# Four-layer sparse graph attention: seven row gathers of the third layer placed behind the gathers of packed queries

## Chip, cores and metric

One core of one Trainium2 chip runs the whole kernel. The metric is device time in microseconds (us). Three runs of the kernel before gave 1655.29, 1661.34 and 1661.87 us, median 1661.34. A profiled execution of the same kernel took 1662.6 us, and its instructions span 1660.9 us, so 1.7 us lie outside the span.

## What is computed

Eight batches of 2048 nodes with 64 features pass through four layers of graph attention over one sparse adjacency matrix (about 1 edge in 500 set, more for the nodes with low numbers). Each layer is `x = x + layer(relu(layernorm(x)))`. The layer concerned here is layer 2, the one with four heads:

```python
mask = graph + jnp.eye(N, dtype=graph.dtype) > 0
h = jnp.einsum('bnc,hdc->bhnd', x, Wh)
out_h = _gat_layer(h, mask[None, None], bh[None, :, None, :])   # softmax(h h^T, masked) h + b
cat = jnp.transpose(out_h, (0, 2, 1, 3)).reshape(B, N, H * D)
z = jax.nn.leaky_relu(cat, negative_slope=0.2)
h2 = jnp.einsum('bnk,dk->bnd', z, Wo)
out2 = _gat_layer(h2, mask[None], bo)                            # then leaky, layernorm, add to x
```

## The kernel before

**Tiles and slots.** The nodes are cut into 16 tiles of 128. The kernel does not form the 2048 x 2048 scores. For tile `i`, each query keeps its first `ROWS[i]` neighbours in slots of its own, and what neighbours are left over are packed, 128 at a time, into `PACKED[i]` further slots. One slot is one indirect DMA of 128 rows (`gather`, L252 to 264, the DMA at L259) from a table in HBM into one of the 26 places of a ring in SBUF (`RING`, `ring`, `held`). A tile has `ROWS[i] + PACKED[i]` slots: 4 each for tiles 8, 9 and 10, 3 each for 12, 11 and 13, and 17 for tile 0.

**The heads' stage of layer 2.** `ORDER2` (L44) names the tiles in the order 8, 9, 10, 12, 11, 13, 0, 7, and so on. `pipeline(take2, first2, second2, third2, fourth2)` at L858 walks over them, tile n being taken while tile n-1 is scored and n-2 is weighed.

- `take2` (L744 to 752) gathers the tile's rows, loads the tile's own rows and its projected queries `q` (1 MB, L751), and asks `fetch` for the first packed queries.
- `fetch` (L735 to 742) sends indirect DMAs `qe` (L740), 128 projected queries of 8,320 bytes each, about 1.06 MB, for the packed slots of all tiles in one stream. There are `QE = 4` buffers, so the fifth `qe` can go only when VectorE has done with the first. Scoring a packed slot asks for the `qe` four places on (L773). What follows call these qe0, qe1, ... : qe0 is that of tile 8, qe1 of tile 9, qe2 of tile 10, qe3 and qe4 of tile 12.
- `score` (L754 to 773): for each slot ScalarE copies the row into PSUM (L763), VectorE multiplies it with the query (L765, 2.28 us), sums over features (L769, 2.29 us) and subtracts (L770), and ScalarE takes the exponential (L771).
- `weights` (L775 to 798), twice a tile: GpSimd multiplies rows by weights (L782, 1.92 us each; L795 adds two such products), TensorE sums them in PSUM (L797); `divided` scales the sums on ScalarE (L805).
- `third2` and `fourth2` project them (L830 to 854, VectorE's part at L451), and store the rows of the table that layer 2's second half gathers from.

The projected queries are made by `products` (L330 to 345), the last stage of layer 1, which stores them into the table `qtab` (L345). A `qe` reads any row of `qtab`, so qe0 must wait until the last tile's store has landed. A row gather of layer 2 must wait for the last store into `table[2]` (L363), which comes earlier.

**What sets the order of the queues.** Each engine runs its instructions in the order of its own queue. That order is fixed when the program is built, by a planner that walks through the program with a clock of its own: of the instructions whose inputs are there by that clock it takes the one that comes first in the program text. An instruction that is not ready is passed over, and later ones go ahead of it. A gather is ready as soon as its table is stored and its place in the ring is free. GpSimd's queue carries all row gathers, all `qe`, and all of L782 and L795.

In layers 1 and 3 the function `additive` already holds gathers back: the gather of tile n waits for the scoring of tile n-3 (`SPREAD`, L516 to 518). In the heads' stage nothing holds them back.

Of the kernel before, what the change touches and what calls it, by code (L numbers as in the profile page):

```python
# [34 lines left out]

PAIRS = [0, 0, 2, 2, 2, 0, 0, 0, 2, 2, 2, 2, 2, 2, 2, 2]
QE = 4

SPREAD = 3

# [21 lines left out]
def edge_stack(ctx: ExitStack, tc: tile.TileContext, x_in, adj, w1, w1t, a1, wh, wht, bh, wo, bo,  # L62
# [9 lines left out]
    nc = tc.nc  # L72
# [143 lines left out]
    order = list(MAKING)  # L216
# [35 lines left out]
    def gather(k, i, st, behind=None):  # L252

        n = SLOTS[i]
        assert sum(SLOTS[j] for j in held) + n <= RING
        held[i], front[0] = front[0], (front[0] + n) % RING
        cols = table[k].shape[1]
        for t in range(n):
            g = nc.gpsimd.indirect_dma_start(  # L259
                out=ring[:, (held[i] + t) % RING, :cols], out_offset=None, in_=table[k][:, :],  # L260
                in_offset=bass.IndirectOffsetOnAxis(ap=idx[:, OFF[i] + t:OFF[i] + t + 1], axis=0))
            if behind is not None and t == 0:
                tc.add_manual_dep(g.ins, behind.ins.name, mybir.DependencyInfo(
                    mybir.DependencyClass.Sync, mybir.DependencyReason.DATA), reason="gather")

    def load(st, name, src, bufs):
        st[name] = rows_pool[0].tile([P, F], F32, name=name, bufs=bufs)
        nc.sync.dma_start(out=st[name], in_=src)

    def rows_of(k, i):  # L270
        return table[k][i * P:(i + 1) * P, :F]
# [452 lines left out]
    with tc.tile_pool(name="l2", bufs=2) as l2p, \  # L724
# [5 lines left out]
        thin[0] = ps_z  # L730

        stream = [(i, t) for i in order for t in range(PACKED[i])]
        sent = {}

        def fetch(upto):  # L735

            while len(sent) <= min(upto, len(stream) - 1):
                i, t = stream[len(sent)]
                q = sent[i, t] = l2p.tile([P, QW], F32, name="qe", bufs=QE)
                nc.gpsimd.indirect_dma_start(  # L740
                    out=q, out_offset=None, in_=qtab[:, :],
                    in_offset=bass.IndirectOffsetOnAxis(ap=qidx[:, POFF[i] + t:POFF[i] + t + 1], axis=0))

        def take2(i, st):  # L744
            gather(2, i, st)
            load(st, "rows", rows_of(2, i), 3)
            if i in order[:2]:
                st["q"] = kept[i]
            else:
                st["q"] = own_pool[0].tile([P, QW], F32, name="q")  # L750
                nc.sync.dma_start(out=st["q"], in_=qtab[i * P:(i + 1) * P, :])  # L751
            fetch(stream.index((i, 0)) + min(PACKED[i], QE) - 1)

        def score(i, st, lo, hi):  # L754

            K, n = ROWS[i], hi - lo
            w = l2p.tile([P, max(ROWS), B * H], F32, name="w2", bufs=5)[:, :n]
            st.setdefault("w", []).append(w)
            s = ps_s.tile([P, F], F32, name="s2")[:, :n * B * H].rearrange("p (t c) -> p t c", c=B * H)
            for t in range(lo, hi):  # L760
                q = st["q"] if t < K else sent[i, t - K]
                g = ps_g.tile([P, F], F32, name="g2")
                nc.scalar.copy(g, row(i, t))  # L763
                pr = l2p.tile([P, B * H, D], F32, name="prod2")
                nc.vector.tensor_tensor(  # L765
                    pr.rearrange("p (b h) d -> p b h d", h=H),
                    q[:, :B * H * D].rearrange("p (b h d) -> p b h d", h=H, d=D),
                    heads(g)[:, :, None, :].to_broadcast([P, B, H, D]), op=OP.mult)
                nc.vector.tensor_reduce(s[:, t - lo, :], pr, AX.X, OP.add)  # L769
                nc.vector.tensor_tensor(s[:, t - lo, :], s[:, t - lo, :], q[:, B * H * D:], op=OP.subtract)  # L770
                nc.scalar.activation(w[:, t - lo], s[:, t - lo], AF.Exp, bias=mbb[:, OFF[i] + t:OFF[i] + t + 1])  # L771
                if t >= K:
                    fetch(stream.index((i, t - K)) + QE)  # L773

# [66 lines left out]
        def fourth2(i, st):  # L841
# [14 lines left out]
            store_rows(3, i, h2, False)  # L856

        pipeline(take2, first2, second2, third2, fourth2)  # L858
        thin[0] = None
    own.close()  # L860
# [543 lines left out]
def whole_stack(tc, t, out):  # L1404
    nc = tc.nc
    D = t["gamma"].shape[0]
    with tc.tile_pool(name="flag", bufs=1) as pool:
        flag = pool.tile([1, 1], I32, name="flag")
        edge_stack(tc, t["x"], t["adj"], t["w1"], t["w1t"], t["a1"], t["wh"], t["wht"], t["bh"], t["wo"],
                   t["bo"], t["gamma"], t["beta"], t["w3"], t["w3t"], t["a3"], out, flag)  # L1410
        bad = nc.values_load(flag, min_val=0, max_val=1)
        with tc.If(bad > 0):
            gnn_stack(tc, t["x"].rearrange("n (b d) -> n b d", d=D), t["adj"], t["w1"], t["a1"], t["wht"],
                      t["bh"], t["wo"], t["bo"], t["gamma"], t["beta"], t["w3"], t["a3"],
                      out.rearrange("n (b d) -> n b d", d=D))
# [36 lines left out]
```

## Time and profile before

| | us |
|---|---|
| Median of three runs | 1661.34 |
| Profiled execution | 1662.6 |
| Its span | 1660.9 |
| VectorE (DVE) busy | 1311.9 (79%) |
| TensorE (PE) busy | 1214.6 (73%) |
| GpSimd (POOL) busy | 1151.1 (69%) |
| ScalarE (ACT) busy | 741.6 (45%) |
| L259, row gathers on POOL, 405 of them | 396.2 busy, 222.4 idle before them |
| L782, row times weight on POOL, 162 of them | 307.3 busy, 30.0 idle before them |
| L740, packed queries on POOL, 32 of them | 0.94 to 0.98 each |

The heads' stage lies between 636 us (its first gather) and 1193 us (the first gather of the next stage). In a timeline line the columns are the start in us, the length in us, the engine, the line of the kernel, the operation, what it writes and reads, the count, and in brackets the idle time ahead of it and what ended that. An indirect DMA shows twice: the POOL instruction (about 0.95 us) that issues it, and the transfer, which lands later.

### The profile page before, as it was taken

What the parts mean: (1) busy time and instruction counts of PE and PEld (TensorE: products, weight loads), DVE (VectorE), ACT (ScalarE), POOL (GpSimd) and SP (SyncE); (2) the same over time, 40 slices, a digit from 0 to 9 for tenths busy, and PEclk for the clock granted to TensorE, in tenths of its full rate; (3) what the DMA queues carried; (4) which work ended last, traced back from release to release, by engine and by line L of the source; (5) the groups of instructions that cost most, each with busy time, mean ns of one, the idle gap of its engine ahead of it and who ended that gap; (6) DMA issues with size and microseconds to landing.
All of it is one profiled execution on the core that took longest, in us unless ns stands there. A gap on an engine that the chain in (4) does not pass through costs nothing. (4 is left out here: it accounts for less than half of the span.)

```text
span 1660.9 us, 15702 instructions
## 1 busy us (share of the span) xinstructions
PE 1214.6 (73%) x3771; PEld 606.7 (37%) x3771; DVE 1311.9 (79%) x2674; ACT 741.6 (45%) x2362; POOL 1151.1 (69%) x903
## 2 busy tenths in 40 slices
PE   0025576776789974599997999999576868846898
PEld 0012243343454541234343344443233424423555
DVE  5978999994669987799999799861179979954667
ACT  5851223443257783356632455554334445560011
POOL 5765866786764215899689889998277889656650
PEclk9998877986889997799999999999877978857899
DMA  5545554453776537656255345300273443126771
GB/s 167 181 163 179 171 191 164 140 193 125 213 256 231 183 157 271 233 180 222 92 202 184 123 142 188 138 13 13 102 259 121 146 127 114 64 77 198 228 213 63
DMA packets 85787, 266.94 MB, mean 161 GB/s; under 512 B 14627, under 2 KB 14659, under 8 KB 75446
## 3 DMA queue, kind: packets, MB, share of 16 engines
q0 software_dynamic: 37328, 141.05, 27.4%
q1 hardware_dynamic: 48358, 124.79, 21.0%
q8 instruction: 32, 0.52, 0.1%
q14 instruction: 69, 0.57, 0.1%
HBM read 208.74 MB, written 57.05 MB: 160 GB/s over the span
## 5 line engine op out<-in xcount | busy, mean ns | idle before, releaser
L259 POOL DMA_INDIRECT g<-table,idx x405 | 396.2, 978 | 222.4 <-issue 131.7
L782 POOL TENSOR_TENSOR wh<-g,w 128x1024 f32<-128x1024 f32 x162 | 307.3, 1917 | 30.0 <-PE y L797 27.9
L394 PE MATMUL y<-wg,ident 128*128 128x512 f32 x392 | 232.4, 720 | 74.4 <-POOL wg L389 67.8
L299 POOL TENSOR_TENSOR ln_r<-ln_q,mhalf 128x8 f32<-128x8 f32 x80 | 135.9, 1702 | 129.0 <-DVE ln_q L297 93.0
L769 DVE TENSOR_REDUCE s<-prod 128x32 f32<-128x2048 f32 x81 | 183.9, 2285 | 14.6 <-ACT w L771 14.4
L389 POOL TENSOR_TENSOR wg<-g,w 128x1024 f32<-128x1024 f32 (+1 forms) x91 | 160.0, 1767 | 39.7 <-ACT w L445 31.7
L797 PE MATMUL y<-wh,ident 128*128 128x512 f32 x320 | 154.3, 609 | 28.1 <-POOL wh L795 24.4
L394 PE MATMUL y<-wg,selt 128*128 128x512 f32 x256 | 142.7, 669 | 6.0 <-POOL wg L389 6.0
L394 PEld LDWEIGHTS y<-wg,ident 128*128 128x128 f32 x392 | 79.6, 223 | 160.4 <-POOL wg L389 82.8
L797 PE MATMUL y<-wh,selt 128*128 128x512 f32 x256 | 124.6, 613 | 10.4 <-POOL wh L782 10.4
L805 ACT ACTIVATE yn<-y,rec 128x64 f32<-128x64 f32 x512 | 110.7, 366 | 27.6 <-PE y L797 26.8
L765 DVE TENSOR_TENSOR prod<-q,g 128x2048 f32<-128x2048 f32 x49 | 111.4, 2274 | 5.2 <-ACT g L763 5.1
L389 DVE TENSOR_TENSOR wg<-g,tiny 128x1024 f32<-128x1024 f32 (+1 forms) x92 | 98.1, 1086 | 12.3 <-PE y L394 11.9
L451 DVE SCALAR_TENSOR_TENSOR zt<-m,bhc,att 128x512 f32<-128x512 f32 x64 | 47.2, 737 | 74.9 <-ACT att L450 74.8
L408 PE MATMUL m<-w,selt 128*128 128x8 f32 (+1 forms) x384 | 61.0, 262 | 54.0 <-ACT w L554 19.1
L408 PEld LDWEIGHTS m<-w,selt 128*128 128x128 f32 x384 | 63.7, 215 | 100.0 <-ACT w L554 26.6
L307 ACT ACTIVATE xh<-x,ln_r 128x64 f32<-128x64 f32 x256 | 88.2, 427 | 25.5 <-POOL ln_r L301 25.4
L797 PEld LDWEIGHTS y<-wh,ident 128*128 128x128 f32 x320 | 58.9, 193 | 104.1 <-issue 64.4
L763 ACT COPY g<-g 128x512 f32<-128x512 f32 x81 | 50.4, 622 | 98.6 <-DVE prod L765 92.6
L437 PE MATMUL q<-rows,sel 128*128 128x512 f32 x128 | 81.4, 739 | 15.4 <-DVE prod L431 8.0
L765 DVE TENSOR_TENSOR prod<-qe,g 128x2048 f32<-128x2048 f32 x32 | 73.0, 2281 | 15.6 <-DMA qe<-qtab,qidx 14.5
L315 PE MATMUL q<-ident,xh 128*128 128x128 f32 x192 | 51.3, 341 | 44.9 <-ACT xh L307 43.1
(208 smaller groups left out, 2593.9 us busy)
## 6 DMA issues: line engine op xcount, KB each, us to landing
qtab<-q SPq DMA_DIRECT2D x16, 1040.0 KB, 4.0
a<-in_adj_dram SPq DMA_DIRECT2D x16, 1024.0 KB, 7.2
q<-qtab SPq DMA_DIRECT2D x14, 1040.0 KB, 5.3
table<-xh SPq DMA_DIRECT2D x48, 256.0 KB, 2.0
rows<-table SPq DMA_DIRECT2D x48, 256.0 KB, 3.8
xs<-x SPq DMA_DIRECT2D x48, 256.0 KB, 2.1
x<-xs SPq DMA_DIRECT2D x48, 256.0 KB, 3.6
table<-xh SPq DMA_DIRECT2D x32, 260.0 KB, 2.4
```

What stands on the lines that cost most here:

```text
L259: g = nc.gpsimd.indirect_dma_start(out=ring[:, (held[i] + t) % RING, :cols], out_offset=None, in_=table[k][:, :], in_offset=bass.IndirectO ...
L299: nc.gpsimd.tensor_tensor(st["rstd"][:, 0, :], q, mhalf, op=OP.pow)
L307: nc.scalar.activation(dst[:, b * D:(b + 1) * D], st["src"][:, b * D:(b + 1) * D], func, bias=0.0 if st["less"] is None else r[:, 1, b:b + ...
L389: eng.tensor_tensor(wg[:, :m].rearrange("p t (b d) -> p t b d", b=B), g[:, :, :F].rearrange("p t (b d) -> p t b d", b=B), w[:, t0:t0 + m, ...
L394: nc.tensor.matmul(y, lhs(i, t), wg[:, t - t0, :], start=(t == 0 and own is None), stop=(t == n - 1))
L408: nc.tensor.matmul(p[:, :cols], selt(i, t), packed[:, t, :], start=(t == 0), stop=(t == T - 1))
L437: nc.tensor.matmul(qe, sel(i, t - K), q, start=True, stop=True)
L765: nc.vector.tensor_tensor(pr.rearrange("p (b h) d -> p b h d", h=H), q[:, :B * H * D].rearrange("p (b h d) -> p b h d", h=H, d=D), heads(g ...
L769: nc.vector.tensor_reduce(s[:, t - lo, :], pr, AX.X, OP.add)
L782: nc.gpsimd.tensor_tensor(wg, heads(row(i, t))[:, :, None, :].to_broadcast([P, B, 2, D]), w[:, :, 2 * k:2 * k + 2, None].to_broadcast([P, ...
L797: nc.tensor.matmul(st["ys"][j], lhs(i, t), wg[:, 4 * j:4 * j + 4], start=False, stop=(t == n - 1))
L805: nc.scalar.activation(yn[:, b, h, :], st["ys"][j][:, b, h, :], AF.Copy, scale=st["rec"][:, 4 * j + b, 2 * k + h:2 * k + h + 1])
```

## The change

The change touches the heads' stage alone. `fetch` now remembers the last `qe` that it issued (`newest`). `take2` notes after each tile which `qe` that was (`lately`). For the third and the fourth tile in the order (n = 2 and 3, tiles 10 and 12), the gathers are written inside `tc.issue_after(...)` of the note left two tiles earlier. `issue_after` is an edge in the queue's order only: the gathers must stand behind that `qe` in GpSimd's queue; they do not wait for it to land. Gathers of the other tiles carry no such edge, and no instruction is added or removed.

```diff
 QE = 4
+LATER = 4
...
-        sent = {}
+        sent, newest, lately = {}, [None], []
 
         def fetch(upto):
...
-                nc.gpsimd.indirect_dma_start(
+                newest[0] = nc.gpsimd.indirect_dma_start(
...
         def take2(i, st):
-            gather(2, i, st)
+
+            n = order.index(i)
+            with tc.issue_after(lately[n - 2].ins) if 2 <= n < LATER else nullcontext():
+                gather(2, i, st)
             load(st, "rows", rows_of(2, i), 3)
...
             fetch(stream.index((i, 0)) + min(PACKED[i], QE) - 1)
+            lately.append(newest[0])
```

At tile 8 `fetch` sends one `qe`, so `lately[0]` is qe0, and the four gathers of tile 10 stand behind qe0. Before tile 9 is taken, the scoring of tile 8's packed slot has asked for four further ones, so `lately[1]` is qe4, and the three gathers of tile 12 stand behind qe4. "Layers 1 and 3 spread" in the change's name is what `SPREAD` does already; it is the same in both kernels.

## Prediction

> **What bounds the kernel now.** The change touches one stage, so I looked first at busy time by stretch of the heads' stage (columns: stretch, length, then PE, PEld, DVE, ACT and POOL busy with counts, granted PE clock, DMA share, GB/s).
>
> ```profile
> 636.00:668.00 32.00, 8.47 (x15) 2.74 (x13) 22.86 (x18) 6.59 (x13) 24.25 (x26) 0.65 0.91 327
> 668.00:684.00 16.00, 2.58 (x3) 1.17 (x4) 7.32 (x5) 1.10 (x2) 12.28 (x10) 0.50 0.82 307
> 684.00:790.00 106.00, 98.23 (x278) 41.97 (x277) 100.78 (x91) 62.75 (x215) 99.36 (x64) 0.99 0.57 192
> 790.00:866.00 76.00, 72.22 (x215) 31.97 (x214) 74.54 (x60) 36.94 (x107) 56.09 (x34) 1.00 0.41 140
> 866.00:943.00 77.00, 61.58 (x146) 25.29 (x145) 64.48 (x55) 26.86 (x86) 70.89 (x49) 0.96 0.48 155
> ```
>
> Read columns DVE and POOL. From 684 to 790 both are full: DVE 100.8 of 106, POOL 99.4. From 790 to 866 DVE alone is full (74.5 of 76), and POOL has 20 us to spare. From 866 to 943 POOL is full. So the stage changes its bound twice. Next I asked the timeline where the start loses time.
>
> ```profile
> 661.91 0.26 DVE L412 TENSOR_REDUCE row<-w 128x32 f32<-128x96 f32 x1 [0.35 <-ACT w L771]
> 676.65 2.29 DVE L765 TENSOR_TENSOR prod<-qe,g 128x2048 f32<-128x2048 f32 x1 [14.48 <-DMA qe<-qtab,qidx]
> ```
>
> ```profile
> 636.13 1.02 POOL L259 DMA_INDIRECT g<-table,idx  x1 [5.75 <-DMA table<-xh]
> ...
> 667.48 0.94 POOL L259 DMA_INDIRECT g<-table,idx  x1 [0.30 <-issue]
> 668.72 0.94 POOL L740 DMA_INDIRECT qe<-qtab,qidx  x1 [0.30 <-issue]
> ...
> 673.42 5.64 POOL L782 TENSOR_TENSOR wh<-g,w 128x1024 f32<-128x1024 f32 x3
> 679.03 2.34 POOL L795 TENSOR_TENSOR wh<-wh 128x1024 f32<-128x1024 f32 x1
> 683.83 0.97 POOL L740 DMA_INDIRECT qe<-qtab,qidx  x1 [2.47 <-DVE s L770]
> 684.83 5.65 POOL L782 TENSOR_TENSOR wh<-g,w 128x1024 f32<-128x1024 f32 x3
> ```
>
> DVE stands still 14.48 us for qe0. Between 636 and 668 POOL issues 26 gathers, 1.25 us apart: the ring's 26 places, tiles 8, 9, 10, 12, 11, 13 (21) and the first five of tile 0. Only then come qe0 to qe3. Was qe0's data there earlier? The waits of SP's queue answer.
>
> ```profile
> SPq L751 <- DVE s L770: 7.4, 1, 7.4
> SPq L751 <- DMA qtab<-q: 3.9, 1, 3.9
> ```
>
> The load at L751 went at 661.59; less 7.4, the last store into `qtab` had landed by 654.2. So qe0 stood in the queue 14.5 us longer than its data asked, as long as DVE's stall.
>
> [...] at 683.83 POOL had stood 2.47 us for DVE's L770. [...] at a DMA share of 0.91 the last `qtab` store took 7.7 us (646.49 to 654.2), where the page of the profile has a median of 4.0. [...] the trace has a median of 6.1 us for a `qe`, but 6.0 to 13.7 for the first five, so I use 7.93 us, from qe0's issue (668.72) to DVE's start (676.65).
>
> **The change part by part.**
>
> *Seven gathers leave the place ahead of qe0.* Four of tile 10, three of tile 12. The other 19 carry no edge, and the trace shows that the planner brings every gather with a free place ahead of a `qe` that isn't ready, even tile 0's. I expect 19 ahead: 636.13 + 19 x 1.25 = 659.9 us for qe0, 8.8 us earlier than 668.72. The store (654.2) is not the limit. DVE starts at 659.9 + 7.93 = 667.8, and its stall is 676.65 - 667.8 = 8.8 us shorter. Bounds: nothing, if the order stays; 14.5 us, if only tiles 8 and 9 stay ahead.
>
> *The seven come back behind.* They are not removed. POOL's queue becomes: 19 gathers to 659.9; qe0 to qe3, 4 x 1.25, to 664.9; tile 10's gathers to 669.9; four L782/L795 operations, 5.64 + 2.34, to 677.9; then qe4. It needs L770 of qe0, which comes 6.9 us after DVE's start (676.65 to 683.56), so at 674.7: POOL no longer waits. With issue, qe4 is done at 679.1, tile 12's gathers take 3.75, and the next L782 starts at 682.8, against 684.83. **POOL gains 2.0 us**, its removed wait of 2.5 less roundings, not 8.8. If tile 12's gathers fall between later products, the first of these starts up to 3.75 us sooner and those after it give that back.
>
> *What is late next.* POOL then runs to 789 with one gap of 0.51 us, issue gaps apart. DVE's lead of 8.8 us can't stay, because ScalarE ties them: the scaled sums (L805), which need POOL's products through PE, stand in its queue ahead of the copies and exponentials that DVE needs. At 716 it shows:
>
> ```profile
> 709.45 0.69 ACT L450 ACTIVATE att<-m,bhl 128x512 f32<-128x512 f32 x1 [0.33 <-PE m L834]
> 716.06 1.74 ACT L805 ACTIVATE yn<-y,rec 128x64 f32<-128x64 f32 x8 [4.01 <-PE y L797]
> 717.64 0.34 ACT L771 ACTIVATE w<-s,mbb 128x32 f32<-128x32 f32 x1
> ```
>
> The exponential at 717.64 already cost DVE 1.27 us (718.01). Part of this chain is DVE's own: L451 at 713.80 reads what ACT had finished at 710.14, PE's L846 waits for it, and PE's packed sum (L797) stands behind L846 at 714.90, while POOL had its product at 712.4 (the first of three from 710.50, 1.92 each). So PE could be 2.4 us earlier without POOL. I take a lead of **2.0 + 2.4 = 4.4 us**; the other 4.4 of the 8.8 return as waits on ACT. From 790 to 866 POOL waits 11.0 us for DVE (`qe`) and 8.0 for PE (L797), so there POOL can make up the 2.4. Beyond 866 both are shifted alike, and the next stage begins when the last row of this one is stored: a shift passes on whole.
>
> *Hidden, costed at nothing.* Tile 10's rows now land by 669.9 + 13.7 = 684 at the latest measured landing; ACT copies the first at 695.57, less 8.8: 686.8. The cover is 3 us; gone, it costs the lateness on DVE. Tile 12's rows (682.8 + 8) are first needed about 714. The edge is no wait; behind qe4 in the queue stand POOL's products, and PE waits for those, but qe4 is ready 3 us before POOL reaches it. SP's queue has nothing moved.
>
> **Sum.** 1662.6 - 4.4 = 1658.2 for the profiled execution. This lies 1.3 above the median of the runs, so against the median: 1661.3 - 4.4 = **1656.9 us**, 0.26% less.
>
> **Rivals.** What a measurement of this kernel can tell from no change is about 0.5%, 8.3 us.
>
> *Full gain.* DVE is the bound and keeps 8.8: 1652.5; up to 14.5 with eight gathers ahead: 1646.8. For it: DVE idles only 5.2 us in 684 to 790. Against: POOL is as full there.
>
> *POOL waits instead: slower.* Place: POOL's queue ahead of qe0. If the planner doesn't bring tiles 11, 13 and 0 forward past the held ones, eight gathers end at 646.1, POOL idles 8.0 us to 654.2, and the 11 gathers (13.75 us) fall into the full stretch. By 789 the same work is done with 8.0 - 2.5 = 5.5 us more idle: 1666.8. It decides from 2.5 us of idle, that is with fewer than 12 gathers ahead (636.1 + 12 x 1.25 = 651.1; 654.2 - 2.5 = 651.7). The same happens if qe4 is placed ahead of the four products. For it: the trace shows hoisting without edges only.
>
> *The planner's order shifts elsewhere.* Seven moved instructions change its clock; ties fall otherwise on PE, ACT and POOL over 530 us. The stall at 912 (9.93 us, DVE for ACT's L771, POOL behind it) shows what one unlucky place costs: 1661 plus or minus 10. The change's own effect is then not what shows.
>
> **How the numbers follow.** Absorbed gain 0.49, centre 1656.9, own range 1652 to 1661. Full gain 0.16, of which 0.11 beyond 8.3 us and 0.04 below 1649. POOL waits 0.20, of which 0.08 above 1669.6, where the idle also hits products that PE needs. Order shifts 0.15, of which 0.03 more than 8.3 us faster and 0.09 more than 8.3 us slower. The forecast's own case reaches past the lower bound with 0.01, since the runs before scatter by 6.6 us. Faster: 0.11 + 0.03 + 0.01 = 0.15; slower: 0.08 + 0.09 = 0.17; same: the other 0.68. The range 1649 to 1669 leaves out 0.04 of full gain and 0.01 of shifts below, and 0.08 of waits and about 0.07 of shifts above, 0.20 in all.
>
> **What would show it.** Right: 19 gathers ahead of the first `qe`, that at about 660; DVE's wait for it 5 to 7 us; a new wait of 4 us in all on ACT's L763 or L771 between 685 and 720; POOL's product that was at 684.83 at 681 to 683. Wrong: fewer gathers ahead with POOL idle before 654; POOL's waits for DVE from 790 to 866 gone by 8 us or more (full gain); DVE's stall unchanged; or layer 2 elsewhere in another order.

## The result, and the profile after

| | us | ratio to the kernel before (95% interval) |
|---|---|---|
| Before, 10 runs | 1661.3 | |
| Changed, 10 runs | 1666.78 | 1.0032 (1.0018 to 1.0046) |
| Forecast | 1656.9 | 0.9974 |

The changed kernel is 0.32% slower, 5.5 us. The time lies inside the range (1649 to 1669), but only because the range also had to hold the rivals: the sign is not the one forecast. The profiled execution took 1668.23 us with a span of 1666.5 us.

The place of the change looks as forecast. First the timeline of the changed kernel on GpSimd (all lines stand one to five numbers later than before):

```profile
633.15 1.02 POOL L260 DMA_INDIRECT g<-table,idx  x1 [6.30 <-DMA table<-xh]
...
655.74 0.94 POOL L260 DMA_INDIRECT g<-table,idx  x1 [0.30 <-issue]
656.98 0.94 POOL L741 DMA_INDIRECT qe<-qtab,qidx  x1 [0.30 <-issue]
...
661.95 0.95 POOL L260 DMA_INDIRECT g<-table,idx  x1 [0.30 <-issue]
...
666.69 5.64 POOL L787 TENSOR_TENSOR wh<-g,w 128x1024 f32<-128x1024 f32 x3
672.29 2.34 POOL L800 TENSOR_TENSOR wh<-wh 128x1024 f32<-128x1024 f32 x1
674.79 0.98 POOL L741 DMA_INDIRECT qe<-qtab,qidx  x1 [0.16 <-issue]
...
679.54 5.65 POOL L787 TENSOR_TENSOR wh<-g,w 128x1024 f32<-128x1024 f32 x3
```

That is: nineteen gathers, qe0 to qe3, four gathers of tile 10, the products, qe4 without a wait, three gathers of tile 12, products. On VectorE the stall for qe0 has gone from 14.48 to 4.83 us:

```profile
665.12 2.29 DVE L770 TENSOR_TENSOR prod<-qe,g 128x2048 f32<-128x2048 f32 x1 [4.83 <-DMA qe<-qtab,qidx]
```

To see where the time is lost I cut both profiled executions at three marks that each timeline shows: the first gather of the heads' stage, the load of `sel` with which the second half of layer 2 starts, and the last store of row maxima, after which only layer 3 is left.

| us | up to the heads | heads' stage | second half of layer 2 | layer 3 |
|---|---|---|---|---|
| before | 636.13 | 556.93 | 306.72 | 161.12 |
| changed | 633.15 | 556.56 | 311.38 | 165.41 |

The heads' stage gains only 0.4 us, and 9 us are lost behind it, where no instruction was touched. (The 3 us ahead of the stage are scatter of single executions: up to there both kernels run the same instructions in the same order.) The two traces also show that the order of the queues differs from the heads' stage on. In the second half of layer 2, counted by source line, VectorE's queue has an instruction of another line in 284 of its 493 places, ScalarE's in 117 of 465, TensorE's in 223 of 580, GpSimd's in 48 of 175. The planner walks through the program with one clock, so seven gathers that it places otherwise can move every later choice.

What that costs is in the groups of VectorE in the second half of layer 2 (busy us and mean ns behind the bar). Before:

```profile
L297 DVE TENSOR_SCALAR ln_q<-ln_q 128x8 f32<-128x8 f32 x32 | 12.7, 396 | 0.2
L280 DVE TENSOR_SCALAR tiny<-ln_s 128x8 f32<-128x8 f32 x32 | 5.1, 159 | 0.0
```

After:

```profile
L298 DVE TENSOR_SCALAR ln_q<-ln_q 128x8 f32<-128x8 f32 x32 | 19.8, 618 | 0.2
L281 DVE TENSOR_SCALAR tiny<-ln_s 128x8 f32<-128x8 f32 x32 | 5.1, 160 | 0.1
```

These are two operations of the same kind on 128x8 values. The one that writes to PSUM (`tiny`) takes 160 ns both times. The one that stays in SBUF (`ln_q`, mean times 1/64 plus epsilon in `norm_b`) takes 396 ns on average before and 618 after, 7.1 us more, on the engine that is busiest there (246.4 us of the 306.7 before). All other groups of VectorE agree within 0.3 us. The mean hides two kinds: 24 of the 32 take 150 to 223 ns before, and 8 take 0.52 to 1.85 us. After, 11 take more than 0.3 us, up to 3.46. The timeline of the changed kernel shows the longest one, all engines together:

```profile
1354.57 0.95 POOL L260 DMA_INDIRECT g<-table,idx  x1 [0.30 <-issue]
1355.02 3.46 DVE L298 TENSOR_SCALAR ln_q<-ln_q 128x8 f32<-128x8 f32 x1
...
1355.53 2.91 POOL L390 TENSOR_TENSOR wg<-g,w 128x512 f32<-128x512 f32 x2
...
1358.39 0.69 DVE L904 TENSOR_TENSOR y<-y,bo_b 128x512 f32<-128x512 f32 x1
```

It begins while GpSimd issues a gather, and ends at 1358.48, when GpSimd's two products have just ended (1355.53 + 2.91 = 1358.44). No wait is shown; the time is booked as busy. The other long ones end in the same way. In the profile of before, 8 of the 32 begin while GpSimd is at a product (L389): they are the 8 long ones, and each ends 26 to 41 ns after a product or a sum of GpSimd has ended. None of the other 24, among them 6 that begin during the issue of a gather, takes more than 223 ns. After, 10 of the 11 long ones end 26 to 40 ns behind a product or a sum, the eleventh (360 ns) with the issue of a gather. `tiny` meets a product as often (10 of 32 both times), and none of the 32 takes more than 171 ns.

The traces show when `ln_q` stands still, not what stops it. Beside GpSimd's other small operation, `ln_r` on 128x8 values (L299, L300), an `ln_q` of this stage that began in the middle of it took at most 174 ns before (8 of them) and 177 after (10). My guess, which the experiments below test, is that `ln_q` stands still while GpSimd is at a product or a sum, and that it would not in a form that also writes an extra sum. If it is so, the order that the planner picks decides how often, and for how long, these small operations meet GpSimd's products.

### The profile page after: what moved, and what is told of

Same layout as the page of the kernel before. It is cut to its first block, busy times and chain, and to the rows that moved or that the text cites. A ratio compares the mean times of both kernels' runs of the same rounds, so it can differ in the third digit from the quotient of the medians.

```text
span 1666.5 us, 15695 instructions
## 1 busy us (share of the span) xinstructions
PE 1229.8 (74%) x3771; PEld 614.1 (37%) x3771; DVE 1325.0 (80%) x2674; ACT 742.6 (45%) x2362; POOL 1152.4 (69%) x903
## 4 chain that ended last, share of the span: by engine, by line
PE 25%; DVE 13%; POOL 7%; ACT 6%; issue 5%; DMA 5%; SPq 0%; POOLq 0%; DVEq 0%; ACTq 0%
PE y L802 10%; PE y L395 5%; POOL g L260 3%; ACT yn L810 3%; DVE s L774 3%; DVE prod L770 3%; PE y L794 2%; PE m L851 2%; DMA g<-table,idx 2%; DMA rows<-table 2%; PE m L839 2%; POOL wh L787 2%; POOL wg L390 1%; POOL ln_r L300 1%; PE m L835 1%
## 5 line engine op out<-in xcount | busy, mean ns | idle before, releaser
L395 PE MATMUL y<-wg,ident 128*128 128x512 f32 x392 | 245.8, 760 | 66.5 <-POOL wg L390 56.2
L300 POOL TENSOR_TENSOR ln_r<-ln_q,mhalf 128x8 f32<-128x8 f32 x80 | 135.9, 1702 | 131.0 <-DVE ln_q L298 95.5
L395 PEld LDWEIGHTS y<-wg,ident 128*128 128x128 f32 x392 | 85.7, 239 | 158.5 <-POOL wg L390 73.6
L390 DVE TENSOR_TENSOR wg<-g,tiny 128x1024 f32<-128x1024 f32 (+1 forms) x92 | 98.1, 1085 | 16.7 <-PE y L395 16.4
L794 PE MATMUL y<-rows,ident 128*128 128x512 f32 x128 | 70.9, 641 | 19.3 <-DMA rows<-table 12.9
L369 POOL TENSOR_TENSOR acc<-acc,xh 128x512 f32<-128x512 f32 x45 | 58.4, 1299 | 31.0 <-ACT xh L308 22.3
```

The costliest lines, as they stand in the source:

```text
L300: nc.gpsimd.tensor_tensor(st["rstd"][:, 0, :], q, mhalf, op=OP.pow)
L390: eng.tensor_tensor(wg[:, :m].rearrange("p t (b d) -> p t b d", b=B), g[:, :, :F].rearrange("p t (b d) -> p t b d", b=B), w[:, t0:t0 + m, ...
L395: nc.tensor.matmul(y, lhs(i, t), wg[:, t - t0, :], start=(t == 0 and own is None), stop=(t == n - 1))
L794: nc.tensor.matmul(st["ys"][j], ident, xb[:, 4 * j:4 * j + 4], start=True, stop=False)
```

## The experiments

All were run on other chips, where the kernel before takes about 1705 us (medians 1703.75 to 1706.62 in four sessions). Every ratio is to the kernel before in the same session, with its 95% interval. To hold an order I chained each engine's instructions of a stage by edges that fix the queue's order only, as `issue_after` does; the order itself is that of the kernel before or of the changed one. The traces show the queues in the order that was asked for:

```diff
+def pinned(tc, nc, text):
+    by = {i.name: i for i in nc.cur_bb.bb.instructions}
+    for steps in json.loads(zlib.decompress(base64.b85decode(text))):
+        names = [n for n in (f"I-{k}" for k in itertools.accumulate(steps)) if n in by]
+        for first, then in zip(names, names[1:]):
+            tc.add_manual_dep(by[then], first, ...)
...
+        pinned(tc, nc, QUEUES)
         bad = nc.values_load(flag, min_val=0, max_val=1)
```

### Which part loses: the move, or the new order behind it

**The seven gathers alone**: kernel before, `QUEUES` its own order with the seven gathers moved in GpSimd's queue.

> Every queue of every engine is in the order of the kernel before; only the seven gathers of tiles 10 and 12 stand where the changed kernel has them in POOL's queue (19 gathers, qe0 to qe3, four gathers, the products, qe4, three gathers). This is the change without any replanning. My forecast, that POOL absorbs most of it: about 4.4 us less than before, 0.997. Full gain: 8.8 us less, 0.995. POOL's unbroken run takes all but its own gap: 2.0 us less, 0.999. If the move itself costs, because the seven gathers now stand between products that PE waits for: 5 us more, 1.003.

Measured: 1703.41 us, 0.9982 (0.9969 to 0.9994). The move by itself gains 3.1 us. The interval (1.0 to 5.3 us) would also hold the forecast's 4.4; what decides between the two are the traces, further down.

**The heads' stage as planned for the change**: changed kernel, `QUEUES` the later stages' order of the kernel before.

> The changed kernel as planned up to the end of the heads' stage; every queue after that (second half of layer 2, layer 3) in the order of the kernel before. Theory replanning of later stages: the loss lies there, so this one is within 2 us of before (0.999 to 1.001), the heads' stage -0.4 us as in the profile after. Rival, POOL or PE loses in the heads' stage: this one carries the whole loss, about 5.5 us more, 1.0032.

Measured: 1705.0 us, 0.9985 (0.9971 to 0.9998), somewhat better than the theory had it. The loss is not in the heads' stage: beside the move alone (0.9982), what the planner changed inside the stage costs nothing that these times can tell.

**The later stages as planned for the change, without the change**: kernel before, `QUEUES` both later stages in the changed kernel's order.

> The kernel before up to the end of the heads' stage, with no gather held; every queue after that in the order of the changed kernel. Theory replanning of later stages: the whole loss with none of the change, 5 to 9 us more than before, 1.003 to 1.0055. Rival, loss in the heads' stage: no difference, 1.000.

Measured: 1712.12 us, 1.0027 (1.0012 to 1.0041), just under the range expected. The loss is there with no gather held.

**Layer 3 alone in the new order**:

> The kernel before, with only layer 3's queues (DVE, ACT, PE) in the order of the changed kernel; the second half of layer 2 as before. By the profiles, layer 3 took 4.3 us more after the change and the second half of layer 2 4.7 us more: if order is the cause in both, 3 to 4.5 us more here, 1.002 to 1.0027; if layer 3's difference is scatter between two executions, none, 1.000.

Measured: 1707.06 us, 0.9999 (0.9986 to 1.0012). Layer 3's order costs nothing that can be told; 4.3 us, by which the two profiles differ there, would be 1.0025, outside the interval. They are scatter of single executions.

**The second half of layer 2 alone in the new order**, and beside it the changed kernel again:

> The kernel before, with only the second half of layer 2 in the order that the planner chose for the changed kernel; the heads' stage and layer 3 as before. Theory (the loss lies in this stage's order): 1.0027, as with the orders of both later stages (1.0012 to 1.0041). Rival (the loss needs layer 3's order or the moved gathers too): below 1.001.

Measured: 1710.37 us, 1.0033 (1.0020 to 1.0046), from five runs.

> The changed kernel once more, beside the three others of this call, as the measure for their ratios: 1.0032 of the kernel before (1.0018 to 1.0046) by every theory, if the chip plays no part.

Measured: 1707.21 us, 1.0014 (1.0003 to 1.0024). It is slower here too, by less; the two intervals overlap. The parts fit it: 0.9985 x 1.0033 = 1.0018.

### What in that order costs: the times of GpSimd's products, or other waits

Here `ln_q` takes the form with an extra sum as second output. The expectations and the labels of the runs call the guess "port" and this form "port-free"; these are names only, since no run shows what stops the operation. The mean's factor goes into ScalarE's square (1/8 squared is 1/64), so that one operation is left for VectorE, beside the reading of the sum. (`sole[0]` is set where the second half of layer 2 begins.) The order of all queues is held, so nothing else differs.

```diff
-            nc.scalar.activation(st["sq"], st["src"], AF.Square)
+            nc.scalar.activation(st["sq"], st["src"], AF.Square, scale=INV_D ** 0.5 if sole[0] else 1.0)
...
-        q = small.tile([P, B], F32, name="ln_q")
+        q8 = small.tile([P, B + sole[0]], F32, name="ln_q")
+        q = q8[:, :B]
...
+        if sole[0]:
+            nc.vector.tensor_scalar(q, q, EPS, None, op0=OP.add, op1=OP.add,
+                                    accum_out=q8[:, B:])
```

> The kernel before in its own order; in the second half of layer 2 the 32 small VectorE operations that write ln_q (mean and epsilon, 128x8) take a form with an extra sum as output, and the factor 1/64 moves into ScalarE's square. Theory, port: these operations stand still while GpSimd works[...]; in the extra-sum form they don't. In the profile of before they take 12.7 us where 32 at the shortest are 5.1, so 7.6 us of VectorE go; about two thirds of such time reached the end (4.6 of 7.1 us), so 5 us less: ratio 0.997. Rival, order alone: the lengths are recorded waits for something else; they stay at a mean near 400 ns and the ratio is 1.000.

Measured: 1700.45 us, 0.9974 (0.9964 to 0.9985). Two operations that begin just behind the start of a product show the difference. The kernel before:

```profile
1297.51 1.90 POOL L389 TENSOR_TENSOR wg<-g,w 128x1024 f32<-128x1024 f32 x1 [1.80 <-ACT w L445]
1297.59 1.85 DVE L297 TENSOR_SCALAR ln_q<-ln_q 128x8 f32<-128x8 f32 x1
```

With the extra sum:

```profile
1317.93 1.90 POOL L398 TENSOR_TENSOR wg<-g,w 128x1024 f32<-128x1024 f32 x1 [1.80 <-ACT w L454]
1318.03 0.15 DVE L303 TENSOR_SCALAR_CACHE_REDUCE ln_q<-ln_q 128x8 f32<-128x8 f32 x1
```

Nine of the 32 begin during a product here, and none of the 32 takes more than 163 ns.

> The changed kernel in its own order, with the same edit. Theory, port: 19.8 us against 5.1, so 14.7 us of VectorE go, about 9.5 of them at the end: ratio 0.997 to 0.998, not above the kernel before with the same edit by more than 0.0005; the loss of the new order is gone. Rival, order alone (waits for rows, ScalarE and TensorE are what makes the new order longer[...]): it stays 0.0025 to 0.003 above the kernel before with the same edit.

Measured: 1699.77 us, 0.9969 (0.9958 to 0.9979). The groups of this second kernel in the stage:

```profile
L285 DVE TENSOR_SCALAR tiny<-ln_s 128x8 f32<-128x8 f32 x32 | 5.2, 161 | 0.1
L304 DVE TENSOR_SCALAR_CACHE_REDUCE ln_q<-ln_q 128x8 f32<-128x8 f32 x32 | 4.9, 154 | 0.2
L304 DVE DVE_READ_ACCUMULATOR ln_q<-ln_q 128x1 f32 x32 | 2.6, 82 | 0.0
```

No long ones are left (107 to 163 ns), and the changed kernel is no longer slower than the kernel before with the same edit. What stops `ln_q` was not shown. What the runs show is that the long ones come with GpSimd's products and sums (18 of the 19 in the profiles of before and after), and that neither `tiny`, with its result in PSUM (at most 171 ns), nor the form with the extra sum (at most 163 ns) has any. The expectation had forgotten the instruction that reads the sum, 82 ns each: 7.5 us in all, not 5.1.

**The new order of the second half of layer 2, with that form**, the sharpest test, since it differs from the kernel of 1.0033 only in the form of these 32 operations, with the reading of the sum and the factor in ScalarE's square:

> The kernel before with only the second half of layer 2 in the changed kernel's order, as in half2_replanned (1.0033), now with the port-free form of ln_q in that stage. Theory, port: the order costs nothing once its small operations don't wait for GpSimd, so it ends where the kernel before with the same edit did: 0.9974, up to 0.9985. Rival (a part of the order's cost lies in other waits, as much as 0.0033): 1.000 to 1.0007; half and half would be 0.999.

Measured: 1701.58 us, 0.9982 (0.9971 to 0.9993). The order's cost falls from 0.0033 to 0.9982 - 0.9974 = 0.0008. So about three quarters of it, by these ratios, was the waiting of these operations. What is left, 1.4 us, lies inside the intervals (together they allow -0.0007 to 0.0023). The changed kernel points the same way: with this form it lies 0.0005 under the kernel before, where the move alone gives 0.0018. Whether a part of the order's cost lies in other waits stays open.

**A third order**: the changed kernel, planned freely, with one number changed.

```diff
-LATER = 4
+LATER = 3
```

> The changed kernel with LATER = 3, planned freely: only tile 10's four gathers stand behind qe0, and the planner makes a third order of everything from the heads' stage on. Own effect: qe0 goes 4 x 1.25 = 5.0 us earlier, so 3.0 x 5.0 / 8.8 = 1.7 us less. Theory, port: what the new order of the second half of layer 2 adds is two thirds of what its 32 ln_q take over 12.9 us there; with 20 us of ln_q it ends at +3.0 us (ratio 1.0018), with 13 us at -1.7 us (0.999), to 2 us. Rival: the order costs by other waits, and the ratio doesn't follow the ln_q time.

Measured: 1706.63 us, 1.0016 (1.0003 to 1.0030), with 18.5 us of `ln_q` in the stage. The expectation's rule, with 0.65 for its two thirds, gives -1.7 + 0.65 x 5.6 = +1.9 us, 1.0011, inside the interval. But it is no more than a rule of thumb. The profile of the second kernel above (`heads_replanned`, old order) shows 16.7 us of `ln_q` and no loss, so not every such wait reaches the end; where VectorE has slack behind it, it may cost nothing, which was not tested. And for the changed kernel, run again, it gives too little: 17.3 us of `ln_q` and the move's 3.1 us make -0.2 us, where 1.0014 was measured.

### A version that beats both

The old order with the seven gathers moved, and the extra-sum form in the second half of layer 2:

> Both gains in one kernel: the order of the kernel before everywhere, only the seven gathers moved, and the port-free form of ln_q in the second half of layer 2. Theory (the two are independent: one lies in the heads' stage, one in the stage behind it): 0.9982 x 0.9974 = 0.9956. Rival (both shorten VectorE, and what one frees the other can't free again): 0.997.

Measured: 1696.3 us, 0.9947 (0.9930 to 0.9965). The two gains add up.

The same, with the form in the earlier stages too (the diff shows `ln_m`; 16 more `ln_q` take the form shown above):

> The same, and also the other 16 centred ln_q and the 32 ln_m of the earlier stages in the port-free form; the orders are held there too. In the profile of before these take 9.5 us for the 32 ln_m, and the 48 ln_q of the earlier stages 12.6 us. The new form was measured at 0.154 + 0.082 us, so ln_m goes to 7.5 and the 16 ln_q save 1 us at most. Theory: at most 2 us less than the kernel above, ratio 0.9945 to 0.9956. Rival (VectorE is not the bound there): the same as the kernel above.

```diff
-        st["less"] = small.tile([P, B], F32, name="ln_m")
-        nc.vector.tensor_scalar(st["less"], s, -INV_D, None, op0=OP.mult)
+        m8 = small.tile([P, B + 1], F32, name="ln_m")
+        st["less"] = m8[:, :B]
+        nc.vector.tensor_scalar(st["less"], s, -INV_D, None, op0=OP.mult, op1=OP.add, accum_out=m8[:, B:])
```

Measured: 1696.21 us, 0.9952 (0.9934 to 0.9970), no difference that can be told; the rival holds.

## Why the prediction was wrong, step by step

**Gathers ahead of qe0.** Right. Nineteen, with qe0 23.8 us after the first gather, as forecast (659.9 - 636.13); the stall for it is 4.83 us, just under the 5 to 7 forecast.

**What POOL gains.** Right. Forecast 2.0 us, the removed wait of 2.5 less roundings. Two runs on one chip, one in the old order there (`layer3_replanned`) and one with the seven gathers moved (`seven_alone`), show the wait for qe4 at 3.10 us before and gone after, and GpSimd's products 2.9 us earlier from there to the end of the stage. The wait varies between executions (2.47 us in the profile of before), and by estimate the gain with it.

**What VectorE keeps beyond it.** This term was wrong: 2.4 us forecast, none measured in that pair. In those two runs' timelines, the start of each of VectorE's sums (L773 there), counted from the first gather of the stage, shows VectorE's lead over the old order: 9.1 us at 44 us into the stage, 4.3 at 60 and 2.9 at 76, and it stays there, within 0.3, to the end. It falls to GpSimd's lead and no further. I had ScalarE as the tie; in this order it is mostly TensorE:

```profile
690.24 2.34 POOL L799 TENSOR_TENSOR wh<-wh 128x1024 f32<-128x1024 f32 x1
...
692.63 5.99 PE L801 MATMUL y<-wh,ident 128*128 128x512 f32 x8 [18.14 <-POOL wh L799]
...
698.46 0.30 PE L412 MATMUL m<-w,selt 128*128 128x32 f32 x2
...
698.80 0.19 DVE L821 SCALAR_TENSOR_TENSOR rec<-m,row 128x32 f32<-128x32 f32 x1 [4.40 <-PE m L412]
```

VectorE needs TensorE's packed sum of weights (L412), 0.3 us of work. It stands in TensorE's queue behind eight matmuls that begin when GpSimd's sum is done. That wait takes 4.40 us, and two small ones for ScalarE 1.12 and 0.37: 5.9 of the 6.2 us that the lead loses. So the gain is 2.9 us in the traces and 3.1 in the times, against 4.4.

In the changed kernel itself, whose stage was laid anew, VectorE is tied otherwise:

```profile
686.27 4.49 DVE L774 TENSOR_REDUCE s<-prod 128x32 f32<-128x2048 f32 x2 [2.27 <-ACT w L776]
700.50 2.29 DVE L770 TENSOR_TENSOR prod<-q,g 128x2048 f32<-128x2048 f32 x1 [0.78 <-ACT g L768]
716.07 0.27 DVE L413 TENSOR_REDUCE row<-w 128x32 f32<-128x96 f32 x1 [0.69 <-ACT w L776]
741.81 0.19 DVE L822 SCALAR_TENSOR_TENSOR rec<-m,w 128x32 f32<-128x32 f32 x1 [2.23 <-PE m L409]
```

Here ScalarE takes 3.7 us between 685 and 720, close to the 4 us that the forecast named as its sign, and TensorE 2.2. That the lead would be lost was right; on which engine depends on the order.

**"A shift passes on whole", with the time after the stage left as it was.** This is the step that failed, and that turned the sign: the sum put a new order of the later stages at nothing. Where the order is held the step is true: 2.9 us all along the stage, 3.1 at the end. But the planner does not hold it. Behind the heads' stage it laid all queues anew, and its order of the second half of layer 2 costs 0.0033, 5.6 us, more than the move gains.

**The rivals.** Full gain and waiting POOL are out: in that pair 9.3 us of stall were removed (15.14 to 5.89) and 2.9 kept, and GpSimd had no idle time ahead of qe0. What happened is the rival that the planner's order shifts elsewhere (0.15), with the absorbed gain beneath it. That rival named places on TensorE, ScalarE and GpSimd; the price was mostly on VectorE, by a wait that no chain of waits shows. Layer 2 "elsewhere in another order" was the last of the signs given for being wrong.

## What to carry to other kernels

When a planner lays out the queues, an edit of one stage is also a new draw for every stage behind it: compare the queues of the two programs first, and hold the old order to measure the edit by itself. Here the draw (1.0033) was larger than the edit (0.9982). Where one group of instructions of equal shape has a mean far above its median (here 396 and 618 ns against 171), look for what another engine is at when the long ones end: here all 8 of before and 10 of the 11 after ended 26 to 41 ns behind a product or a sum of GpSimd, and their time was booked as busy time, not as a wait.

## What the runs showed of the hardware

- A `tensor_scalar` of 128x8 from SBUF to SBUF (`ln_q`) took 150 ns to 1.85 us in the profile of before, 119 ns to 3.46 us in that of after, and up to 4.25 us in `later_replanned`. The one that writes to PSUM (`tiny`) took 159 and 160 ns on average before and after. With the extra sum `ln_q` took 107 to 163 ns in `port_free_before` and `port_free_after` (mean 154 both times), 155 and 156 ns on average in `half2_port_free` and `seven_port_free`; reading the sum took 82 to 84 ns.
- The `ln_q` that began at 1355.02 in the profile of after ended at 1358.48: it did not end between GpSimd's instructions, but lasted through the rest of a gather's issue (to 1355.52) and the two products that followed (1355.53 to 1358.44).
- The lengths belong to the order in the main, not wholly: the 32 took 12.7, 13.1, 13.1 and 16.7 us in four executions of the old order of that stage (two of the eight longest of the last, 2.16 and 2.34 us, are short in the others), and 17.3 to 20.9 us in four of the new order.
